# Last stage of a two-layer kernel: selection by partition quadrants in two halves, with the first half's ranks as sums of signs

## The chip, the cores and the metric

The kernel runs on one core of a Trainium2 chip. A core has a matrix engine (PE, TensorE), a vector engine (DVE, VectorE), an activation engine (ACT, ScalarE), a general engine (POOL, GpSimd) and a synchronising engine (SP, SyncE). Each works through its own list of instructions in order, and they wait for one another through semaphores. Transfers are issued from SP, ACT or POOL and carried out by shared DMA engines. The metric is the device time of one execution in microseconds (us), median of several runs; lower is better.

## The reference

Four sequences of 1024 tokens with 256 numbers each pass through two layers: windowed attention, a mixture of eight experts with two chosen per token, full attention with its own normalisation, and at last the stage that is changed here. That stage lets each of 8 experts choose 128 of the 1024 tokens of each sequence:

```python
B, N, D = x.shape
E = gate_w.shape[-1]
M = N // E
gate_logits = jnp.einsum('bnd,de->bne', x, gate_w)
competitive_gates = sinkhorn(gate_logits)
vals, idx = jax.lax.top_k(jnp.swapaxes(competitive_gates, -1, -2), M)
...
routed = x[b_idx, routed_indices]
...
outputs = jnp.einsum('ebmd,edf->ebmf', routed, experts)
outputs = outputs * jnp.transpose(gate_values, (2, 0, 1))[..., None]
vals_bmed = jnp.transpose(outputs, (1, 2, 0, 3))
routed_back = jnp.zeros_like(x).at[b_idx, routed_indices].set(vals_bmed)
```

`sinkhorn` divides the gates eight times by their sums over tokens and over experts. The input is normalised per token before the stage, and `x` is added to `routed_back` after it. Where several experts have chosen one token, the last one's row is what is kept; the kernel takes the highest expert number.

## The kernel before

The tokens are 32 tiles of 128, held in `x_t`. The last stage treats the sequences in two groups of two: group 0 is tiles 0 to 15, group 1 tiles 16 to 31. A group has 16 pairs of (sequence, expert), called columns here, and each column chooses 128 tokens.

For each group these steps follow. `gate_steps` (L1014) normalises the tiles, writes them to `xn_d` in DRAM for later gathers, turns them on PE and multiplies by the gate weights. `share_steps` (L1064) does the eight rounds of division. `choose_steps` (L1088) copies the gates to `by_tile`, turns them so that each column is one partition of `cur` (16 partitions of 1024 numbers), and then runs 16 rounds on DVE. A round has three instructions: the eight largest values (L1109, `max`), their places (L1111, `max_index`), and a copy in which they are struck out (L1115, `match_replace`). Values and places are turned back, so that slot s of a column lies on partition s (`slot_gate`, `slot_tok`, `slot_row`).

`experts_on` (L1135) gathers the rows of each column by an indirect DMA from POOL into `xg`, turns them (L1181, copied by ACT at L1185), multiplies by the expert's matrix (L1154), scales by the gate on ACT (L1164) and writes them to `y_d` from SP (L1168). To return the results, each token must know its slot. For group 0 the slots are scattered to `rank_d` in DRAM by `ranks` (L1585 and after) while attention still runs. For group 1 they are made on chip: DVE compares each place with the chosen token (L1832, `hot`), and PE multiplies this with slot numbers, `slot_col` (L1834). `back` (L1194) turns the slots into row numbers, gathers the rows of `y_d` into `yr` (L1225, POOL), adds `x` (L1231, POOL for group 0, DVE for group 1) and writes the output from SP (L1232).

Group 0's gates and selection are steps of a generator that is interleaved with the second attention: after each half of an attention step, `some` takes a step of the waiting jobs, and a selection step only if nothing else was done or at every fourth attention step. `finish` normalises the attention's results, the last tile's too (L1559 to L1564, on POOL). Group 1's gates complete only when the last attention tile is through. The last stage then runs group 1's division and selection, with group 0's experts and returns beside it, and then group 1's experts, ranks and returns.

Each engine's order is made by a scheduler from its own estimate of times, within the orders that the code demands. `paced` adds a wait on another instruction; `issue_after` asks for a place behind another one. Hardware DMAs, issued from SP and ACT alike, take turns on eight semaphores in the scheduled order, and the compiled order shows a wait for the transfer that used the same semaphore before. POOL's DMAs have eight of their own.

Of the kernel before, what the change touches and what calls it, by code (L numbers as in the profile page):

```python
# [8 lines left out]
F32 = mybir.dt.float32  # L9
# [30 lines left out]
def two_layers(  # L40
# [521 lines left out]
    with ExitStack() as lc:  # L562
# [30 lines left out]
        for k in range(2):  # L593
            t = pool.tile([P, D], F32, tag="yr0", name="sb3_k", bufs=7)
            nc.gpsimd.dma_start(out=t, in_=sb3[k].partition_broadcast(P))
            if k == 0:
                nc.gpsimd.tensor_scalar(sb3_b, t, 0.5, None, ALU.mult)
            else:
                nc.gpsimd.tensor_scalar(t, t, 0.5, None, ALU.mult)
                nc.gpsimd.tensor_tensor(sb3_b, sb3_b, t, ALU.add)  # L600
# [413 lines left out]
    def gate_steps(i0: int, i1: int, bank, lag: int):  # L1014
# [7 lines left out]
        for t in range(i0, i1):  # L1022
            xn = gpool.tile([P, D], F32, tag="xng", name="xng", bufs=4)
            nc.gpsimd.tensor_scalar(
                xn, x_t[t], mv_all[:, t, 0:1], rstd_all[:, t : t + 1], ALU.subtract, ALU.mult
            )
            nc.gpsimd.dma_start(out=xn_d[t // TB][(t % TB) * P : (t % TB + 1) * P, :], in_=xn)
            xns.append(xn)
            yield 0
# [58 lines left out]
    def choose_steps(g: int, bank, chosen, after):  # L1088

        by_tile = gpool.tile([P, TB, GE], F32, tag="by_tile", name="by_tile", bufs=1)  # L1090
        nc.vector.tensor_copy(
            by_tile.rearrange("p t (b e) -> p t b e", b=GB),
            gates[:, g * GT : (g + 1) * GT, :].rearrange("p (b t) e -> p t b e", b=GB),
        )
        yield 0
        cur = gpool.tile([GE, S], F32, tag="cur", name="cur")
        for hf in range(2):
            ps = bank()
            for t in range(TB // 2):
                nc.tensor.transpose(  # L1100
                    ps[:GE, t * P : (t + 1) * P], by_tile[:, hf * TB // 2 + t, :], ident
                )
            nc.vector.tensor_copy(cur[:, hf * 512 : (hf + 1) * 512], ps[:GE, :])
            yield 1
        top_v = gpool.tile([GE, CAP], F32, tag="top_v", name="top_v", bufs=1)
        top_i = gpool.tile([GE, CAP], U32, tag="top_i", name="top_i", bufs=1)
        for k in range(CAP // 8):
            eight = slice(8 * k, 8 * k + 8)
            nc.vector.max(out=top_v[:, eight], in_=cur)  # L1109
            yield 0  # L1110
            nc.vector.max_index(out=top_i[:, eight], in_max=top_v[:, eight], in_values=cur)  # L1111
            yield 0
            if k < CAP // 8 - 1:
                nxt = gpool.tile([GE, S], F32, tag="cur", name="cur")
                nc.vector.match_replace(  # L1115
                    out=nxt, in_to_replace=top_v[:, eight], in_values=cur, imm_value=-1.0
                )
                cur = nxt
                yield 0
        top_f = gpool.tile([GE, CAP], F32, tag="top_f", name="top_f", bufs=1)  # L1120
        nc.vector.tensor_copy(top_f, top_i)
        ps = bank()
        nc.tensor.transpose(ps[:, :GE], top_v, ident[:GE, :GE])
        nc.tensor.transpose(ps[:, GE : 2 * GE], top_f, ident[:GE, :GE])
        slot_gate = gpool.tile([P, GE], F32, tag="slot_gate", name="slot_gate", bufs=1)
        nc.vector.tensor_copy(slot_gate, ps[:, :GE])
        slot_tok = gpool.tile([P, GE], F32, tag="slot_tok", name="slot_tok", bufs=1)
        nc.vector.tensor_copy(slot_tok, ps[:, GE : 2 * GE])
        slot_row = gpool.tile([P, GE], I32, tag="slot_row", name="slot_row", bufs=1)
        nc.vector.tensor_copy(slot_row, slot_tok)  # L1130
        chosen[g] = slot_gate, slot_tok, slot_row
        after()
        yield 1

    def experts_on(g: int, pool, chosen, w_all, beside=None):  # L1135

        slot_gate, _, slot_row = chosen[g]
        rows = {}

        def gather(m: int):  # L1140
            for n in (2 * m, 2 * m + 1):
                xg = rows[n] = pool.tile([P, D], F32, tag="xg", name="xg", bufs=6)
                nc.gpsimd.indirect_dma_start(
                    out=xg[:, :],
                    out_offset=None,
                    in_=xn_d[g * GB + n // E][:, :],
                    in_offset=bass.IndirectOffsetOnAxis(ap=slot_row[:, n : n + 1], axis=0),
                )

        def product(m: int, xgT):  # L1150
# [10 lines left out]
            for h in range(2):  # L1161
# [6 lines left out]
                nc.sync.dma_start(out=y_d[g * GB + b][e * CAP : (e + 1) * CAP, :], in_=yg)  # L1168


        gather(0)
        gather(1)
        last = None
        for m in range(GE // 2 + 1):
            if m < GE // 2:
                ps = one_bank()
                for h in range(2):
                    xg = rows.pop(2 * m + h)
                    for kc in range(2):
                        c = (2 * h + kc) * P  # L1180
                        nc.tensor.transpose(  # L1181
                            ps[:, c : c + P], xg[:, kc * P : (kc + 1) * P], ident
                        )
                xgT = pool.tile([P, 4, P], F32, tag="xgT", name="xgT", bufs=3)
                nc.scalar.copy(xgT.rearrange("p k t -> p (k t)"), ps)  # L1185
                if m + 2 < GE // 2:
                    gather(m + 2)
                if beside is not None:
                    beside(m)
# [4 lines left out]
    def back(g: int, rank, order: str, queue, rows):  # L1194
# [3 lines left out]
        def t3(name):  # L1198
            return gpool.tile([P, GT, E], F32, tag=name, name=name, bufs=1)
# [3 lines left out]
        nc.vector.tensor_tensor(key, key, expert_no.to_broadcast([P, GT, E]), ALU.add)  # L1203
        best = gpool.tile([P, GT, 1], F32, tag="best", name="best", bufs=1)
        nc.vector.tensor_reduce(best[:, :, 0], key, AX.X, ALU.max)
        nc.vector.tensor_tensor(key, key, best.to_broadcast([P, GT, E]), ALU.is_equal)
        nc.vector.tensor_tensor(rank, rank, first_slot.to_broadcast([P, GT, E]), ALU.add)
        nc.vector.tensor_tensor(key, key, rank, ALU.mult)
        taken = gpool.tile([P, GT], F32, tag="taken", name="taken", bufs=1)
        nc.vector.tensor_scalar(taken, best[:, :, 0], E - 0.5, None, ALU.is_gt)  # L1210
        src_f = gpool.tile([P, GT], F32, tag="src_f", name="src_f", bufs=1)
# [6 lines left out]
        src_row = gpool.tile([P, GT], I32, tag="src_row", name="src_row", bufs=1)  # L1218
        nc.vector.tensor_copy(src_row, src_f)
        for j in range(GT):  # L1220
            b, t = divmod(j, TB)
            n = j if order == "bt" else t * GB + b
            i = g * GT + j
            yr = rows.tile([P, D], F32, tag=f"yr{g}", name="yr", bufs=8)
            nc.gpsimd.indirect_dma_start(  # L1225
                out=yr[:, :],
                out_offset=None,
                in_=y_d[g * GB + b][:, :],
                in_offset=bass.IndirectOffsetOnAxis(ap=src_row[:, n : n + 1], axis=0),
            )  # L1230
            (nc.vector if g else nc.gpsimd).tensor_tensor(yr, yr, x_t[i], ALU.add)  # L1231
            queue.dma_start(out=out_rows[i * P : (i + 1) * P, :], in_=yr)  # L1232
# [21 lines left out]
    with ExitStack() as lc:  # L1254
# [285 lines left out]
        def finish(i0: int, ys):  # L1540
# [16 lines left out]
            for j in range(n):  # L1557
                x = x_t[i0 + j]
                nc.gpsimd.tensor_scalar(  # L1559
                    ys[j], ys[j], mv[:, j, 0:1], rstd[:, j : j + 1], ALU.subtract, ALU.mult  # L1560
                )
                nc.gpsimd.tensor_tensor(ys[j], ys[j], gamma_b, ALU.mult)
                nc.gpsimd.tensor_tensor(ys[j], ys[j], beta_b, ALU.add)
                nc.gpsimd.tensor_tensor(x, x, ys[j], ALU.add)  # L1564
# [20 lines left out]
        def ranks():  # L1585

            slot_tok = chosen[0][1]
# [68 lines left out]
        def fetch(i: int, k: int, behind=None):  # L1656

            yr = pools["yr"].tile([P, D], F32, tag="yr0", name="yr0", bufs=7)
# [134 lines left out]
    with ExitStack() as lc:  # L1793
# [6 lines left out]
        nc.gpsimd.iota(place_i, pattern=[[1, S]], base=0, channel_multiplier=0)  # L1800
# [3 lines left out]
        slot_i = wpool.tile([P, GE], I32, name="slot_i")  # L1804
        nc.gpsimd.iota(slot_i, pattern=[[0, GE]], base=1, channel_multiplier=1)
        slot_col = wpool.tile([P, GE, GE], BF16, name="slot_col")
        nc.gpsimd.memset(slot_col, 0.0)
        nc.gpsimd.tensor_copy(
            slot_col.rearrange("p n m -> p (n m)")[:, :: GE + 1], slot_i
        )  # L1810
# [4 lines left out]

        run(share_steps(1, one_bank, 0))

        choose = choose_steps(1, one_bank, chosen, lambda: None)
        for _ in range(3):
            next(choose)  # L1820
        experts_on(0, pool, chosen, w_all)
        for _ in range(24):
            next(choose)
        back(0, read_ranks(), "bt", nc.sync, pool)
        run(choose)
        rank_ps = two_banks()

        def hot_rows(e: int):
            slot_tok = chosen[1][1]
            for n in (2 * e, 2 * e + 1):  # L1830
                hot = pool.tile([P, S], BF16, tag="hot", name="hot", bufs=3)
                nc.vector.tensor_scalar(hot, place, slot_tok[:, n : n + 1], None, ALU.is_equal)  # L1832
# [56 lines left out]
```

## Time and profile before

| | us |
|---|---|
| median of 3 runs | 2508.23 (2507.6 to 2517.59) |
| profiled execution, its time | 2505.83 |
| span of its trace | 2504.1 |
| last attention output copied (L1782) | 2338.14 |
| first selection round of group 1 (L1109) | 2381.85 |
| `slot_row` of group 1 (L1130) | 2441.84 |
| first gather of group 1's return (L1225) | 2477.94 |

The last five times are positions in the trace, counted from its start. The table below is the busy time of the engines in four stretches of the end, in us, with the granted clock of PE as a share of full speed.

| stretch | PE | DVE | ACT | POOL | PE clock |
|---|---|---|---|---|---|
| 2300 to 2350 | 37.82 | 7.82 | 27.79 | 27.55 | 0.80 |
| 2350 to 2400 | 27.23 | 34.60 | 10.44 | 23.97 | 0.65 |
| 2400 to 2450 | 7.40 | 46.34 | 1.89 | 29.97 | 0.59 |
| 2450 to 2505 | 23.95 | 14.94 | 11.43 | 26.39 | 0.74 |

Read it by stretch: in the third, DVE works nearly all the time and the others little; in the fourth no engine is busy for half of it. The trace names instructions by line, engine, operation and tile. "Idle before" is the time that the engine stood still ahead of an instruction, with what released it.

### The profile page before, as it was taken

To read this page: it belongs to the slowest core of one execution; us is meant where nothing else is said; L and a number is where in the kernel's file an instruction comes from. 1 tells how busy PE (TensorE), PEld (TensorE's weight loads), DVE (VectorE), ACT (ScalarE), POOL (GpSimd) and SP (SyncE) were. 2 spreads that over 40 slices of the span, in tenths; PEclk is the share of its full clock that TensorE was granted. 3 is DMA by queue.
4 is the path that set the end of the run, shared out by engine and by line. 5 is a ranking of instruction groups with operands and counts; after the bars stand their busy time and mean duration, and the time that the engine had idled before them with its cause. 6 is when DMAs were issued, how large, how long until landed. Compare 5 with 4: busy or idle time off the path is not lost.

```text
span 2504.1 us, 42234 instructions
## 1 busy us (share of the span) xinstructions
PE 2273.6 (91%) x16844; PEld 1352.2 (54%) x16844; DVE 1392.9 (56%) x2304; ACT 985.6 (39%) x1354; POOL 632.2 (25%) x728
## 2 busy tenths in 40 slices
PE   6999999799999999999888999999999999998434
PEld 3566666566557888887444444444444444443222
DVE  5455545524321222222476877777777798995393
ACT  1333333312111222222114666666666565666311
POOL 2233333510440000000333221212122211124455
PEclk8999999899999999999999999999999999999667
DMA  3000000420116666664515221313121313100144
GB/s 93 19 11 11 11 13 9 133 74 1 66 63 200 217 206 209 213 207 156 117 44 120 59 69 45 69 45 69 45 69 45 69 44 69 44 19 11 56 122 135
DMA packets 201744, 204.90 MB, mean 82 GB/s; under 512 B 90200, under 2 KB 162392, under 8 KB 201548
## 3 DMA queue, kind: packets, MB, share of 16 engines
q1 hardware_dynamic: 179148, 162.13, 22.7%
q0 software_dynamic: 11584, 29.72, 4.0%
q10 hardware_dynamic: 10816, 10.36, 1.2%
q8 instruction: 133, 2.18, 0.4%
q14 instruction: 63, 0.52, 0.1%
HBM read 140.70 MB, written 56.96 MB: 79 GB/s over the span
## 4 chain that ended last, share of the span: by engine, by line
PE 69%; DVE 16%; issue 6%; ACT 4%; POOL 3%; DMA 3%; SPq 0%; DVEq 0%; ACTq 0%; POOLq 0%
PE two L962 10%; PE two L1471 9%; PE acc L1486 8%; PE two L717 6%; DVE tops L1436 5%; PE two L329 5%; PE two L1429 4%; PE acc L989 4%; PE two L258 3%; PE two L1351 2%; PE two L321 2%; PE acc L735 2%; PE misc L735 2%; PE acc L396 2%; PE misc L440 1%
## 5 line engine op out<-in xcount | busy, mean ns | idle before, releaser
L1436 DVE TENSOR_REDUCE tops<-two 128x2 f32<-128x1024 f32 x512 | 619.5, 1217 | 103.8 <-PE two L1429 101.6
L1479 ACT ACTIVATE pT<-two 128x1024 f32<-128x1024 f32 x512 | 523.4, 1025 | 303.7 <-PE two L1471 299.2
L1486 PE MATMUL acc<-pT,v_t 128*32 128x256 f32 x4096 | 342.7, 393 | 5.8 <-ACT pT L1479 5.6
L1471 PE MATMUL two<-q_st,k_st 64*128 64x512 f32 x1024 | 259.8, 499 | 19.3 <-ACT pT L1479 11.8
L962 PE MATMUL two<-xbT,w_t 128*128 128x256 f32 (+1 forms) x1280 | 260.0, 358 | 1.3 <-ACT xbT L951 0.7
L717 PE MATMUL two<-xnT_f,w_t 128*128 128x512 f32 x512 | 234.7, 608 | 7.4 <-DVE tops L1436 5.1
L962 PEld LDWEIGHTS two<-xbT,w_t 128*128 128x128 f32 x1280 | 224.1, 192 | 32.0 <-ACT xbT L951 5.3
L1429 PE MATMUL two<-k_st,q_st 64*128 64x512 f32 x1024 | 220.3, 403 | 4.2 <-DVE glu L726 1.6
L1471 PEld LDWEIGHTS two<-q_st,k_st 64*128 64x128 f32 x1024 | 96.8, 184 | 209.8 <-issue 118.8
L1659 POOL DMA_INDIRECT yr<-ys_d,slot x64 | 62.6, 979 | 573.5 <-DMA w_raw<-in_L_attn_wk_dram 434.7
L1471 PE MATMUL two<-top_st,minus 64*128 64x512 f32 x1024 | 206.5, 396 | 0.0
L978 DVE SCALAR_TENSOR_TENSOR glu_b<-two,b_blk,act_b 128x256 f32<-128x256 f32 (+1 forms) x160 | 72.6, 453 | 235.8 <-ACT act_b L972 235.8
L972 ACT ACTIVATE act_b<-two,b_blk 128x256 f32<-128x256 f32 (+1 forms) x160 | 72.1, 451 | 312.6 <-PE two L962 161.1
L1486 PEld LDWEIGHTS acc<-pT,v_t 128*32 128x32 f32 x4096 | 86.5, 108 | 166.1 <-issue 142.8
L717 PEld LDWEIGHTS two<-xnT_f,w_t 128*128 128x128 f32 x512 | 96.7, 195 | 116.4 <-issue 104.4
L989 PE MATMUL acc<-w_t,glu_b 128*128 128x256 f32 x568 | 148.6, 390 | 8.0 <-DVE glu_b L978 3.7
L355 DVE TENSOR_REDUCE top<-two 128x4 f32<-128x768 f32 (+1 forms) x128 | 112.5, 919 | 69.0 <-PE two L329 69.0
L381 POOL TENSOR_SCALAR_AFFINE_SELECT pT<-pT 128x1024 f32<-128x1024 f32 x64 | 70.5, 1102 | 296.5 <-ACT pT L378 296.5
L725 ACT ACTIVATE act<-two,bT 128x512 f32<-128x512 f32 x64 | 44.0, 687 | 254.0 <-PE two L717 251.2
L1429 PEld LDWEIGHTS two<-k_st,q_st 64*128 64x128 f32 x1024 | 103.2, 185 | 73.5 <-ACT pT L1479 22.0
L378 ACT ACTIVATE pT<-two 128x768 f32<-128x768 f32 (+1 forms) x128 | 93.7, 783 | 119.0 <-PE two L329 118.6
L989 PEld LDWEIGHTS acc<-w_t,glu_b 128*128 128x128 f32 x568 | 102.1, 189 | 34.7 <-DVE glu_b L978 23.3
(317 smaller groups left out, 3095.0 us busy)
## 6 DMA issues: line engine op xcount, KB each, us to landing
w_t<-in_L_ffn_rw_dram SPq DMA_DIRECT2D x120, 512.0 KB
halves<-split SPq DMA_DIRECT2D x64, 256.0 KB
q_st<-halves SPq DMA_DIRECT2D x128, 128.0 KB
k_st<-halves SPq DMA_DIRECT2D x256, 64.0 KB
xb<-xs_d SPq DMA_DIRECT2D x31, 256.0 KB
ys_d<-yb ACTq DMA_DIRECT2D x31, 256.0 KB
xs_d<-zeros SPq DMA_DIRECT2D x5, 1536.0 KB
b_t<-in_L_ffn_rb_dram SPq DMA_DIRECT2D x40, 128.0 KB
```

Of the source, the lines that this page charges most:

```text
L329: mm(parts[r][:, gg, :], lhsT=left[32 * r : 32 * r + rows, g, l0 : l0 + P], rhs=right[32 * r : 32 * r + rows, g, r0 : r0 + n], start=(mask ...
L355: nc.vector.tensor_reduce(tops[i][:, 2 * ab : 2 * ab + 2, 2 * gp : 2 * gp + 2], scs[ab], AX.X, ALU.max)
L378: nc.scalar.activation(pt[:, 2 * ab : 2 * ab + 2, :, :n], scs[ab], AF.Exp)
L717: mm(ps[:, n * 512 : (n + 1) * 512], lhsT=w_t[:, kc, f * P : (f + 1) * P], rhs=xnT[:, kc, cols], start=(kc == 0), stop=(kc == 1),)
L735: mm(ps[:, jj * D : (jj + 1) * D], lhsT=glu[:, f, j * P : (j + 1) * P], rhs=w3_t[:, f, :], start=(f == 0), stop=(f == NF - 1),)
L962: mm(ps[:, m * 512 + ff * cols : m * 512 + (ff + 1) * cols], lhsT=w_t[:, kc, f * P : (f + 1) * P], rhs=xbT[:, kc, :cols], start=(kc == 0), ...
L989: mm(ps[:, a * D : (a + 1) * D], lhsT=glu[:, f, a * P : (a + 1) * P], rhs=w3_t[:, f, :], start=(f == 0), stop=(f == NF - 1),)
L1429: mm(sc[:, hh], lhsT=q_st[rows, j * P : (j + 1) * P], rhs=k_st[rows, kk * 512 : (kk + 1) * 512], start=True, stop=True,)
L1436: newest["vector"] = nc.vector.tensor_reduce(tops[:, :, j, kk], sc, AX.X, ALU.max).ins
L1471: mm(sc[:, hh * 512 : (hh + 1) * 512], lhsT=minus[rows] if top else k_st[rows, k * P : (k + 1) * P], rhs=(top_ring[p % 2] if top else q_st ...
L1479: newest["scalar"] = nc.scalar.activation(pt, sc, AF.Exp).ins
L1486: newest["tensor"] = mm(oT_ps[32 * r : 32 * r + 32, hh * D : (hh + 1) * D], lhsT=vals[n // HU][:, n % HU, k, :], rhs=pts[r // 2][:, hh * 5 ...
```

## The change

**Selection by quadrants.** The gates are turned twice side by side, so that 32 partitions hold the 16 columns doubled. A round now reads one of 16 places (four quadrants of 32 partitions, four positions in each) and `match_replace` writes the next place. The values of every round stay, so the places are found afterwards for four rounds, or two, at once: `max_index` over 128 partitions for group 0 and 64 for a half of group 1.

**Two halves for group 1.** After eight rounds the first 64 slots of each column are turned, gathered (8 gathers, each of two columns' half) and run through `half_experts`, whose products are 64 slots wide; then the same for the other 64.

**Ranks.** For the first half ACT computes the sign of (place - token + 0.5) and PE adds these with weights of half a slot number; the difference of neighbouring places, made by four products with `ident` and `minus`, is the slot number at the chosen place. The second half's ranks are made by DVE comparisons as before and added to the same sums. They are read out per sequence.

**Moved.** Results go to `y_d` from ACT instead of SP, 16 writes for group 0 and 32 of half size for group 1. Group 0's returns are issued in three lots (7, 7, 2), each behind a lot of gathers in POOL's order. All 16 gathers of group 0's experts stand ahead of the division of group 1. The last tile's normalisation steps and its `xng` go from POOL to DVE. Buffers: `xg` 16 for 6, `yr` 16 for 8 per group, `yr0` 6 for 7.

```diff
-            nc.gpsimd.tensor_scalar(
-                xn, x_t[t], mv_all[:, t, 0:1], rstd_all[:, t : t + 1], ALU.subtract, ALU.mult
-            )
+            last_xn[:] = [
+                (nc.gpsimd if lag else nc.vector)
+                .tensor_scalar(
...
-        cur = gpool.tile([GE, S], F32, tag="cur", name="cur")
+        cur = gpool.tile([P, 4, S], F32, tag="cur", name="cur", bufs=1)
...
-        for k in range(CAP // 8):
-            eight = slice(8 * k, 8 * k + 8)
-            nc.vector.max(out=top_v[:, eight], in_=cur)
-            yield 0
-            nc.vector.max_index(out=top_i[:, eight], in_max=top_v[:, eight], in_values=cur)
-            yield 0
...
+        def of_round(k: int):
+            return slice(32 * (k // 4), 32 * (k // 4) + 32), k % 4
...
+        for k in range(rounds):
+            q, a = of_round(k)
+            behind(nc.vector.max, out=top_v[q, a, :], in_=cur[q, a, :])
             yield 0
...
+            if k + 1 < rounds:
+                q1, a1 = of_round(k + 1)
+                behind(
+                    nc.vector.match_replace,
+                    out=cur[q1, a1, :], in_to_replace=top_v[q, a, :], in_values=cur[q, a, :],
+                    imm_value=-1.0,
+                )
                 yield 0
...
+            if (k + 1) % (rounds // parts):
+                continue
+            part = (k + 1) * parts // rounds - 1
+            rows = slice(part * P // parts, (part + 1) * P // parts)
+            for a in range(4):
+                behind(
+                    nc.vector.max_index,
+                    out=top_i[rows, a, :], in_max=top_v[rows, a, :], in_values=cur[rows, a, :],
+                )
+                yield 0
+            behind(nc.vector.tensor_copy, top_f[rows], top_i[rows])
...
+                        with ExitStack() as order:
+                            if part:
+                                order.enter_context(tc.issue_after(newest["ranks"]))
+                            mm(
+                                ps[row : row + 32, k0 * n : (k0 + 1) * n],
+                                lhsT=top[q].rearrange("p a i -> p (a i)"),
+                                rhs=ident[q, 32 * j + h : 32 * j + GE : parts],
...
-                nc.sync.dma_start(out=y_d[g * GB + b][e * CAP : (e + 1) * CAP, :], in_=yg)
...
+                nc.scalar.dma_start(out=y_d[g * GB + b][e * CAP : (e + 1) * CAP, :], in_=yg)
...
+    def half_experts(g: int, part: int, m: int, xgs, pool, w_all):
...
+        for c in range(2):
+            for kc in range(2):
+                for h in range(2):
+                    half = slice(64 * h, 64 * h + 64)
+                    mm(
+                        ps[half, c * D : (c + 1) * D],
+                        lhsT=xgT[:, 2 * c + kc, half],
+                        rhs=w_all[:, (2 * (m + c) + h) % E, kc, :],
...
+            for h in range(2):
+                row = ((2 * (m + c) + h) % E) * CAP + 64 * part
+                nc.scalar.dma_start(
+                    out=y_d[g * GB + b][row : row + 64, :], in_=yg[64 * h : 64 * h + 64, :]
+                )
...
+        xgs0 = take_rows(chosen[0, 0], columns, pool)
         run(share_steps(1, one_bank, 0))
...
+        choose = choose_steps(1, one_bank, chosen, lambda: ready.append(0), 2)
+        for _ in range(4):
             next(choose)
...
+            if part:
+                nc.vector.tensor_scalar(hot, place, tok, None, ALU.is_equal)
+            else:
+                nc.scalar.activation(hot, place, AF.Sign, bias=half_less[:, m : m + 1])
...
+        some_back(7)
+        while not ready:
+            next(choose)
...
+        xgs = take_rows(chosen[1, 0], columns, pool)
+        for m in range(0, E, 2):
+            half_experts(1, 0, m, xgs[m : m + 2], pool, w_all)
+            for c in range(2):
+                ranks_of(0, m + c)
+            next(choose)
+        for b in range(GB):
+            nc.scalar.copy(sums_to[32 * b : 32 * b + E, 1:], rank_ps[32 * b : 32 * b + E, :])
...
+        some_back(7)
         run(choose)
...
+        xgs = take_rows(chosen[1, 1], columns, pool)
+        some_back(2)
...
+            for m in range(b * E // 2, (b + 1) * E // 2, 2):
+                for c in range(2):
+                    ranks_of(1, m + c)
+                half_experts(1, 1, m, xgs[m : m + 2], pool, w_all)
...
+        with tc.issue_after(newest["numbers"]):
+            for b in range(GB):
+                for t in range(TB):
+                    back(GB + b, t, src_rows[b], t, nc.vector, nc.sync, pool)
```

In the order that the scheduler makes of it, POOL has the seven first returns of group 0, then the 8 gathers of the first half, then seven returns, the 8 gathers of the second half, two returns, and the 16 returns of group 1. PE has the products that turn the second half's values and places behind the last rank product of the first half.

## Prediction

> **What bounds the kernel now.** I read the whole page first (PE is busy for 91% of the span, but the last slices show a single engine each), then the chain of waits in the last 265 us, then the engines' timelines there. The chain:
>
> ```profile
> 2381.14 0.69 DVE cur L1103
> 2381.85 1.23 DVE top_v L1109
> 2383.10 1.27 DVE top_i L1111 x2
> 2384.38 1.21 DVE cur L1115
> 2385.61 1.23 DVE top_v L1109
> ...
> 2442.17 0.76 DVE hot L1832
> ...
> 2459.23 0.96 PE two L1834 x4
> ...
> 2477.94 0.94 POOL yr L1225
> ...
> 2497.00 3.69 DMA yr<-y_d,src_row
> ```
>
> Columns are start, length, piece. From 2381.85 to 2442.0 (60.2 us) only DVE's rounds count, 3.76 us each: values, places, strike-out, about 1.25 us apiece. From there to 2477.94 (35.9) come 16 gathers, experts and ranks at 3.3 us per pair of columns. The returns end it: 16 gathers, 1.25 us apart, and 6.2 for the last to land and leave (26.2 together). What is won must come from the first two stretches.
>
> **Attention, group 0's selection.** Its 16 + 16 + 15 = 47 instructions become 16 + 15 + 4 = 35. The compiled order keeps the same slots for the first 35 and drops the last twelve. DVE is 90% busy there, but only pieces on the chain pay:
>
> ```profile
> 2243.08 1.12 DVE top_v L1109
> 2244.20 2.25 DVE tops L1436 x2
> 2246.45 0.11 DVE rec L1507
> 2246.57 1.20 DVE top_i L1111
> ```
>
> Of the twelve, three lie on it (with 2253.95): 3.5 us. The rank scatters (L1597) then come earlier; two of them, 1.06 and 1.08 us, lie on POOL's chain at 2291.87 and 2298.08. I take 1.5 of about 2.6 with their gaps. Sum **-5** (bounds -1 and -9; the small reordering where attention begins is within that).
>
> **The last tile.** On POOL its four steps and `xng` took 1.23 + 0.74 + 0.72 + 0.73 and 1.24. On DVE the rows for these shapes are 0.45 and 0.42, but the second step still waits for gates at 2350.75. That leaves -1.4, and a second copy of `by_tile` gives back 0.2. POOL's new preparation and its 16 gathers fit beside the 21 us of division. If they did not, group 0's experts would start late, beside DVE's rounds, at no loss. Group 1's first round starts at 2381.85 - 1.2 = 2380.65.
>
> **Selection alone.** First half: 8 x 2.52 + 4 x 1.25 + 0.25 = 25.5, to 2406.1. The turn on PE takes 0.65, and two instructions of the sort (2.5) stand before `slot_row`: 2408.9. Second half: 15 x 1.25 + 0.8 of small copies + 5.25 brings DVE to 2431.1, and `slot_row` could be ready at 2432.3, ten us before today. Searching 64 partitions instead of 16 costs nothing if columns set the price: L1436 takes 1.22 us for 128 x 1024, L1109 1.21 for 16 x 1024. No row shows a strike-out that writes another quadrant; 0 is taken, +0.2 each would be +6.
>
> **POOL's queue.** Seven returns with adds took 13.7 us from 2397.12 in before's timeline. Now: 7 returns from 2396.4 to 2410.0; 8 gathers to 2420.0; 7 returns to 2433.7. So POOL alone would delay the second half's gathers by only 1 us.
>
> **ACT's queue is the added wait.** The writes to `y_d` now stand among ACT's Signs and copies, and each waits for the transfer that last used its semaphore. By the compiled order these are shared with SP's output writes: the fourth write of the first half's first pair waits for the first output of the second lot of seven, later ones for its third to seventh. POOL starts that lot only at 2420.0. The nearest row is SP's queue of today:
>
> ```profile
> 2399.62 0.84 ACT L1164 ACTIVATE yg<-two,slot_gate 128x256 f32<-128x256 f32 x2 [0.85 <-ACT xgT L1185]
> ...
> 2406.16 0.87 SPq L1168 DMA_DIRECT2D y_d<-yg  x2
> ```
>
> The results were ready at 2400.5 and left at 2406.16, behind output writes; only SP stood. The Trainium skill ("DMA: Bandwidth & Descriptors", Anatomy of one DMA) says that a semaphore wait is taken by the issuing sequencer before dispatch. By this rule ACT stands, and with it the Signs behind; the row shows such a wait only on SP, where nothing was behind. Issue costs 0.37 (rows: 0.350 for SP's 128-row writes, 0.417 for ACT's larger L1003).
>
> By the rule: three Signs (1.03, as L1479) end at 2412.2, the first pair is scaled at 2418, and the fourth write stands until 2420.0 + 6.25 + 0.74 + 2.5 for landing = 2429.5. Behind it: nine writes 3.3, three Signs 3.1, two pairs of scalings 1.7, a copy 0.6, and about 1.4 of waiting for PE: 2439.6. Then a copy 0.6, two Signs 2.1 and the last rank products 1.0: **2443.3**. PE's order puts the second half's turn behind those products, so `slot_row` comes at 2443.3 + 1.2 = 2444.5, not 2432.3: **+2.5** against today's 2442.0, before the gain in attention. Without the wait the last product would be at 2433.2.
>
> **Second half to the returns.** Gathers from 2444.8 to 2454.8; two returns of group 0 to 2460.1; their outputs land at 2462.5, and the last two writes of sequence 2 wait for them, land at 2465.5. First return gather 2465.8: 21.3 us behind `slot_row` instead of 35.9, **-14.6**. Sequence 3 (writes 2472.2, row numbers 2472.7) is ready before POOL needs it at 2475.8. Returns and end: 26.2 as today.
>
> **The 64-wide products.** A call has 16 PE records:
>
> ```profile
> 2120.24 1.97 PE L1391 MATMUL misc<-wv_t,xnT_a 128*64 128x128 f32 x32
> 2122.13 0.50 PE L1471 MATMUL two<-q_st,k_st 64*128 64x512 f32 x2
> ```
>
> That is 0.053 us per 128-row record, so 0.107 at 256 rows, 1.7 us a call; L1154's pitch of 0.216 would give 3.5. "TensorEngine Tiling (Array Packing)" (Tiling Modes, Key Properties) speaks against it: changing the mode drains PE. In the row the next shape starts before the modelled end of the last. By the row 0, by the rule one record's 0.27 for each of 16 changes, 4.3 in all, half of it on the path. I take the row: gathers at 2.5 us per pair cover 1.7 + 0.6 + 1.0.
>
> **Sum.** 2504.1 + 2.5 - 14.6 = 2492.0; -5: a span of 2487.0. With the 1.7 outside the span: **2489**, against the profiled 2505.83 (the median shown is 2508.23, 0.1% above it). About 0.5%, some 12.5 us, is what can be told from no change here.
>
> **Rivals.** (A) The forecast, 0.50.
>
> (B) The semaphore waits do not bite, because the writes land earlier or the lots fall otherwise: last rank product 2433.2, POOL ready, span 2478.7 - 5, time **2475**. For it: SP's writes land in 2.4 us at best. Against: the second lot lies behind 8 gathers. 0.18.
>
> (C) Products of 64 columns run one after another with a drain (3.8 a call) and ACT's issue costs 0.5: PE and ACT set the second half, returns from 2472.7 and 2483.8, span 2500.0 - 5, time **2497**. For it: L1154's pitch and a clock of 0.59 to 0.74. Against: L1391. 0.20.
>
> (D) Slower: ACT becomes the bound by its writes. 32 of them stand in series with scalings. At 1.48 us each (SP's longest row, below) the writes of sequence 3 land at 2499.4, the returns wait, span 2516.0 - 5, time **2513**; it is slower than before from 1.25 us a write, and by over 0.5% from 1.7 (2519).
>
> ```profile
> L1168 SPq DMA_DIRECT2D y_d<-yg x32: 319/350/1478, 2386.3 to 2474.8; - x32
> L1003 ACTq DMA_DIRECT2D ys_d<-yb x40: 352/417/427, 783.9 to 1186.1; - x40
> ```
>
> (min/median/max in ns.) Against: ACT's own row never exceeds 0.43. 0.12.
>
> **Numbers.** Range 2474 to 2506: B and C whole, the bounds of attention, a strike-out at +0.2; D is left out. Faster takes most of A, all of B and some of C: 0.64. Same: the rest of A and most of C, half of D: 0.27. Slower: the upper part of D and what I do not see: 0.09.
>
> **What would show it.** In the new trace: 31 instructions 1.25 us apart without `max_index` between; ACT idle for about 11 us behind its fourth half-size write, released by an output DMA; the second half's turn released by a rank product and not by DVE; first return gather 21 us behind the second `slot_row`; calls of 1.7 us on PE. Attention should end about 5 us earlier. I am wrong if ACT does not stand there (B), if PE's products set the pace (C), or if a write on ACT costs over 1.2 us (D).

## The result: 0.4% slower, and the profile after

The changed kernel took 2521.95 us (median of 20 runs, 2510.13 to 2535.43); the kernel before took 2509.39 on the same chip (20 runs). The ratio is 1.0045, with a 95% interval from 1.0028 to 1.0062. The forecast was 2489, in a range from 2474 to 2506. Run once more beside other kernels (e6 below), the ratio was 1.0040 (1.0021 to 1.0059), so the loss of some 10 us is clear of the noise, though small.

The profiled execution of the changed kernel took 2526.09 us, its span is 2524.0. I cut both traces at two marks that both have: the first and the last of the 32 copies to `oT` in the attention stage (L1782 before, L1865 after).

| | before | after | after, again (e6) |
|---|---|---|---|
| start to first `oT` copy | 1367.4 | 1380.2 | 1371.4 |
| attention: first to last `oT` copy | 970.8 | 980.1 | 979.9 |
| last stage: last `oT` copy to the end | 166.0 | 163.7 | 163.6 |

The first row holds almost no changed code, and over all the profiles below it lies anywhere between 1354.9 and 1380.2: it is noise of single executions (e1 to e3, which leave that code alone, have 1362 to 1364 there). The other two rows repeat within 0.2 us in these two traces; attention does not always (986.0 in e3, with the same order of instructions; see there). So in these traces **attention is 9 us longer and the last stage only 2 us shorter**; the forecast had -5 and -12. The two add up to 7 us, the low end of what the times over all runs say (7 to 16).

The last stage first. These are lines of the chain of waits of the changed kernel (start, length, piece; the sort of group 1 begins at 2403.67):

```profile
2403.67 1.23 DVE top_v L1132
2404.92 1.29 DVE cur L1132 x2
...
2452.10 0.33 SPq L1313
...
2452.84 2.19 DMA out_dram<-yr
2455.11 0.48 ACTq L1270
...
2472.55 7.04 PE two L1973 x8
2479.59 1.80 PE two L1949 x4
...
2497.53 0.33 POOL yr L1306
```

The rounds of the sort are shorter, as meant (2.57 us each, with no index search between). But the chain doesn't stay on VectorE: it goes through an output write of SP, a `y_d` write of ACT, and eight products on TensorE (L1973, the difference of the sums) before the returns begin. ACT's own timeline shows the first of these (start, length, engine, line; in brackets the idle time of the engine before, its DMA issues counted as idle, and what ended it):

```profile
2444.45 8.00 ACTq L1270 DMA_DIRECT2D y_d<-yg  x4
2452.50 1.15 ACT L1946 ACTIVATE hot<-place,half_less 128x1024 bf16<-128x1024 f32 x1 [7.71 <-DMA out_dram<-yr]
```

Four writes take 8.0 us, because one of them waits for an output of the second lot of returns to land. At the median of 0.61 us for the issue of such a write (last section), some 2.4 of the 8.0 are issue and 5.6 the wait. ACT computes nothing for 7.71 us ahead of the Sign behind it, and the rank products and the second half's turn stand behind the Sign. The forecast had this wait in it. What it hadn't is in the attention stage.

There, let a *pair* be the time from one `oT` copy to the next. Most of the 31 pairs agree to 0.3 us. These don't, besides 7, 11 and 15:

| pair | before | after | e4: group 0 chosen whole | e9: attention of before |
|---|---|---|---|---|
| 1 + 2 | 56.4 | 58.7 | 58.7 | 56.4 |
| 23 | 41.9 | 44.0 | 43.5 | 41.9 |
| 24 + 25 + 26 | 89.7 | 93.8 | 89.7 | 89.7 |
| 27 + 28 | 61.7 | 59.8 | 62.9 | 61.7 |
| 29 + 30 + 31 | 94.1 | 94.2 | 94.0 | 94.0 |

(Pairs 7, 11, 15 and 23 jump by some 1.5 us between executions of the same code, so one such jump proves nothing. The jumps go with the granted clock: pair 7 took 38.97 us at a clock of 1.00 before and 40.57 at 0.96 after, pair 11 took 40.44 at 0.96 before and 39.04 at 1.00 after. Pair 23 had 1.00 before and 0.96 after; e4, with 0.96 there too, took 43.5 without any quadrants, so most of pair 23's +2.1 is clock.) In pairs 22 to 28 VectorE does group 0's selection beside the attention's row maxima. Pairs 24 to 26, before and after, in one line each (start:end length, busy time and number of instructions of each engine, granted clock of PE, DMA):

```profile
core 0: us, PE busy (x) PEld busy (x) DVE busy (x) ACT busy (x) POOL busy (x), PEclk, DMA share, GB/s
2092.65:2182.33 89.68, 83.70 (x772) 39.16 (x770) 83.68 (x113) 57.60 (x65) 23.19 (x28) 1.00 0.18 47
2112.49:2206.31 93.82, 84.24 (x772) 39.17 (x770) 86.88 (x111) 57.63 (x65) 23.19 (x28) 1.00 0.17 45
```

The clock is full in both. VectorE is busy 3.2 us longer with *fewer* instructions, TensorE hardly longer, and TensorE's weight loads wait for VectorE's maxima for 14.4 us instead of 9.6. VectorE's timeline of the changed kernel, early and late in this selection, shows why:

```profile
2066.23 1.23 DVE L1517 TENSOR_REDUCE tops<-two 128x2 f32<-128x1024 f32 x1 [0.25 <-PE two L1510]
2067.37 1.20 DVE L1132 MAX8 top_v<-cur 32x8 f32<-32x1024 f32 x1
2068.51 1.20 DVE L1517 TENSOR_REDUCE tops<-two 128x2 f32<-128x1024 f32 x1
...
2116.93 2.35 DVE L1517 TENSOR_REDUCE tops<-two 128x2 f32<-128x1024 f32 x2
2119.30 1.22 DVE L1132 MAX8 top_v<-cur 32x8 f32<-32x1024 f32 x1
2120.55 1.23 DVE L1517 TENSOR_REDUCE tops<-two 128x2 f32<-128x1024 f32 x1
```

Add start and length. The reduction at 2066.23 ends at 2067.46, and the max began at 2067.37: they overlap by 0.09 us, and so do the next two (0.06). Fifty us later, with the same shapes, the reduction ends at 2119.28 and the max starts at 2119.30; the max ends at 2120.52 and the next starts at 2120.55. The overlap has turned into a gap, on both sides. Over all 35 selection instructions it is sharp: the first seven, on partitions 0 to 31, have -0.07 before and behind; from the eighth (the first strike-out that writes partitions 32 to 63) to the 31st nearly every one has +0.03 on both sides; the four index searches at the end, which start on partition 0 again, have -0.08 behind them. The Trainium skill ("VectorE: DVE Perf Modes", Two Vector instructions with no wait between them) has the rule: an instruction whose input or output starts in another quadrant of 32 partitions than the last one that used that memory is held until all earlier ones have finished. The gaps agree. The neighbours here start at partition 0, so each selection instruction in quadrants 1 to 3 is held, and so is what follows. As an estimate from the gaps, 24 instructions x 2 x 0.105 = 5 us of VectorE. Pairs 24 to 26 have 16 of the 24, 3.4 us; VectorE was busy 3.2 us longer there, and the pairs grew by 4.1.

### The profile page after: what moved, and what is told of

It is laid out like the page before. It is cut to its first block, busy times and chain, and to the rows that moved or that the text cites. A ratio compares the mean times of both kernels' runs of the same rounds, so it can differ in the third digit from the quotient of the medians.

```text
span 2524.0 us, 42458 instructions
## 1 busy us (share of the span) xinstructions
PE 2306.4 (91%) x16968; PEld 1362.4 (54%) x16968; DVE 1377.0 (55%) x2276; ACT 997.9 (40%) x1369; POOL 629.3 (25%) x730
## 5 line engine op out<-in xcount | busy, mean ns | idle before, releaser
L1510 PEld LDWEIGHTS two<-k_st,q_st 64*128 64x128 f32 x1024 | 103.6, 186 | 80.1 <-ACT pT L1560 21.3
```

What stands on the lines that cost most here:

```text
L1510: mm(sc[:, hh], lhsT=q_st[rows, j * P : (j + 1) * P], rhs=k_st[rows, kk * 512 : (kk + 1) * 512], start=True, stop=True,)
```

## The experiments

Theory H: the loss is made of these holds in attention and of losses in the last stage (ACT's wait, and the eight products). Rival C: it is the granted clock, or something that no edit of these parts moves. Each ratio is against the kernel before on the same chip, with its 95% interval.

| | attention | last stage | ratio |
|---|---|---|---|
| e1 writes on SP | 981.3 | 160.2 | 1.0049 (1.0030 to 1.0067) |
| e2 difference on VectorE | 981.4 | 160.8 | 1.0027 (1.0013 to 1.0042) |
| e3 both | 986.0 | 154.6 | 1.0022 (1.0004 to 1.0039) |
| e4 group 0 whole | 976.6 | 164.3 | 1.0030 (1.0016 to 1.0043) |
| e5 e3 with attention of before | 970.9 | 159.8 | 0.9963 (0.9943 to 0.9983) |
| e7 e4 on partitions 32 to 47 | 989.5 | 167.1 | 1.0061 (1.0039 to 1.0083) |
| e8 before, six `yr0` | 974.4 | 166.6 | 1.0011 (0.9987 to 1.0035) |
| e9 after, attention of before | 970.8 | 164.2 | 1.0003 (0.9988 to 1.0018) |
| e10 e9, writes on SP, turn first | 970.8 | 152.7 | 0.9944 (0.9925 to 0.9964) |
| e11 e5, subtraction later | 970.9 | 149.1 | 0.9931 (0.9904 to 0.9958) |
| e12 e11, eight `yg` | 973.6 | 149.7 | 0.9949 (0.9928 to 0.9970) |
| e13 before, 16 KB `cur` | 973.4 | 166.2 | 1.0028 (1.0004 to 1.0052) |

### e1: `y_d` writes back on SP

```diff
-                nc.scalar.dma_start(out=y_d[...
+                nc.sync.dma_start(out=y_d[...
```

> The changed kernel, with every y_d write (16 whole ones of group 0, 32 half ones of group 1) issued by SP again instead of ACT. Theory L (last stage: the forecast gain is given back there, most of it by ACT): the 8.0 us that ACT stands at a y_d write and the 0.6 us of each issue go, so the last rank product of the first half ends some 10 us sooner, slot_row of the second half follows the selection's own end (about 53 us after the first Max instead of 65.3), and the time falls by 8 to 12 us against the changed kernel, to about the time before. Rival C (the loss is granted clock or sits in the attention stage, and the last stage has other cover): less than 3 us. Rival S (SP's queue now stands at output writes, and the y_d writes behind them come late): no gain or a loss, with y_d writes landing later than now.

The last stage lost 3.5 us, not 8 to 12, and the time didn't move. ACT did stop standing at output writes, and the sums were ready for L1973 at 101.7 us after the last `oT` copy instead of 112.2. But the planner had now put the eight products *ahead* of the second half's turn on TensorE, so `slot_row` came at 109.4 us after the last copy, as before the edit (108.8). The test was spoilt by an order that the edit moved; e10 holds that order fixed.

### e2: the difference taken on VectorE

```diff
-        for hf in range(2):
-            for k, one in enumerate((ident, minus)):
-                mm(rank_ps[:RB, ...], lhsT=one[:RB, :RB], rhs=sums_to[...], ...)
+                if m == 0:
+                    step = pool.tile([RB, S], F32, tag="step", name="step", bufs=1)
+                    nc.vector.tensor_tensor(step, sums_to[:, 1:], sums_to[:, :S], ALU.subtract)
...
-            nc.scalar.copy(rankT[mine], rank_ps[mine, :])
+            nc.vector.tensor_tensor(rankT[mine], rank_ps[mine, :], step[mine], ALU.add)
```

> The changed kernel, with the 8 true-fp32 products by ident and minus (7.04 us on TensorE in the trace) replaced by one subtraction on VectorE of the sums at two neighbouring columns, added to the second half's counts at the read-out (by VectorE instead of ScalarE's copy). Same result. Theory L: TensorE is free 7 us sooner for the second half's experts; of that 3 to 6 us reach the end, as the gathers of the second half (10.0 us) and ScalarE's 16 half writes then bound it. Rival C: under 2 us.

2.9 us of last stage, at the edge of what was expected. ACT stood 7.33 us as in the changed kernel, and `slot_row` stayed at 108.7.

### e3: both

> Both edits together: y_d writes on SP, and the subtraction on VectorE instead of 8 products. Theory L: the two losses follow one another on one chain (ACT, then TensorE), so they add: 12 to 17 us under the changed kernel, which is 2 to 6 us under the kernel before. Rival C: within 3 us of the changed kernel.

The last stage lost 9.1 us, more than e1 and e2 together, though less than the 12 to 17 expected; the time stayed above the kernel before, since attention still carried its loss. Its 986.0 is 5.9 us more than in the changed kernel, with the same order of instructions on TensorE, VectorE, ACT and POOL: in pairs 23 to 28 VectorE was busy 174.74 us against 174.20, but the granted clock was 0.94 against 0.99 and TensorE was busy 192.23 against 183.62. So one trace's attention can differ by 6 us by the clock alone. One more wait showed on VectorE:

```profile
2441.28 1.24 DVE L1132 FIND_INDEX8 top_i<-top_v,cur 64x8 uint32<-64x1024 f32 x1
2450.14 1.22 DVE L1980 TENSOR_TENSOR step<-sums_to 40x1024 f32<-40x1024 f32 x1 [7.62 <-ACT sums_to L1967]
2451.39 0.18 DVE L1132 CAST top_f<-top_i 64x32 f32<-64x32 uint32 x1
```

My subtraction was planned ahead of the cast that ends the sort, and VectorE stood 7.62 us for sums that the sort has no need of. e11 mends that.

### e4: group 0 chosen whole again

```diff
-                    choose_steps(0, misc_bank, chosen, chose)
+                    choose_whole(0, misc_bank, chosen, chose)
```

(`choose_whole` is the `choose_steps` of before, in the space of the new `cur`.)

> The changed kernel, with group 0's selection (the one inside the attention stage) done as before: 16 rounds of max, place and strike-out on 16 partitions, 47 VectorE instructions instead of 35; group 1 and all else as in the changed kernel. My forecast's step (12 fewer instructions give 5 us): 5 us slower than the changed kernel. Theory A (the quadrant form costs the attention stage about 9 us, as the intervals between pairs in the two profiles seem to say): 7 to 10 us faster. Theory N (VectorE's selection has cover in the attention stage, and the difference of the profiles is clock): within 2 us.

Attention fell from 980 to 976.6, and the ratio from 1.0040 to 1.0045 down to 1.0030: between Theory N and Theory A, and against the forecast's step. Pairs 24 to 26 went back to 89.7 us, the value of before; pairs 27 and 28 gave 3.1 back, as the twelve more instructions run there (1.9 by the kernel before, 61.7; the rest is clock: 0.97 there in e4, 1.00 in the other two). Pairs 1 and 2 kept their 58.7.

### e7: the same on other partitions

```diff
-        cur = both[:GE, 0, :]
+        cur = both[32 : 32 + GE, 0, :]
```

(and `top_v`, `top_i`, `top_f` likewise)

> e4 (group 0 chosen whole, 47 instructions) with nothing changed but the partitions: the 16 rows and their tops stand on partitions 32 to 47 instead of 0 to 15. Theory H (an instruction that starts in another quadrant than its neighbours starts only when they have ended, and so does the one behind it): the gap in front of and behind nearly all 47 turns from -0.07 us to +0.03, 47 x 2 x 0.10 = 9 us of VectorE, and pairs 23 to 28, where VectorE is busy over 90%, get some 5 to 9 us longer than in e4. Rival (the quadrant form loses by its semaphores, its strike-out in place or its 32 rows): gaps and pairs as in e4.

This is the decisive pair. The two kernels have the same instructions in the same stage, and differ by 32 partitions. VectorE's timeline in e4:

```profile
2102.36 0.40 DVE L1676 BATCH_NORM_STATS2 st<-y 128x6 f32<-128x256 f32 x1
2102.69 1.20 DVE L1206 MAX8 cur<-cur 16x8 f32<-16x1024 f32 x1
2103.82 0.15 DVE L1677 BATCH_NORM_AGGREGATE mv<-st 128x2 f32<-128x6 f32 x1
```

and the same three in e7:

```profile
2122.33 0.40 DVE L1676 BATCH_NORM_STATS2 st<-y 128x6 f32<-128x256 f32 x1
2122.77 1.22 DVE L1206 MAX8 cur<-cur 16x8 f32<-16x1024 f32 x1
2124.02 0.18 DVE L1677 BATCH_NORM_AGGREGATE mv<-st 128x2 f32<-128x6 f32 x1
```

From first to third start it is 1.46 us in e4 and 1.69 in e7. Attention grew by 12.9 us, more than the 5 to 9 expected. Pairs 23 to 28 show why, e4 first and e7 below:

```profile
2044.40:2240.48 196.08, 185.41 (x1548) 86.87 (x1548) 176.31 (x234) 118.64 (x134) 30.06 (x36) 0.98 0.17 44
2062.57:2272.57 210.00, 191.89 (x1548) 89.36 (x1548) 184.92 (x234) 118.62 (x134) 30.16 (x36) 0.95 0.16 41
```

VectorE is busy 8.6 us longer, close to the 9 us of holds. TensorE is busy 6.5 us longer for the same products, and the clock fell from 0.98 to 0.95: as an estimate, 0.05 x 210 less 0.02 x 196 is 6.6 us of clock lost, which leaves some 7 of the 13.9 us by which these pairs grew. The times over all runs say the same: the two ratios differ by 0.0031, some 8 us, though their intervals leave 1 to 14. The gaps go with the quadrant and not with the semaphores, the strike-out or the number of rows, which e4 and e7 share.

The clock in pairs 23 to 28 is 0.94 to 0.99 in the six traces with holds there (after, e1 to e3, e6, e7) and 0.98 to 1.00 in the others. Whether the holds bring it down or chance does, no run tried.

### e8 and e13: pairs 1 and 2

```diff
-            yr = pools["yr"].tile([P, D], F32, tag="yr0", name="yr0", bufs=7)
+            yr = pools["yr"].tile([P, D], F32, tag="yr0", name="yr0", bufs=6)
```

> The kernel before with one edit: six yr0 buffers instead of seven (the change gave one up for the larger cur). Theory Y (the second pair of the attention stage, 28.1 us before and 32.0 us in every kernel with six, waits for a yr0 buffer): pairs 1 and 2 together 58.8 us instead of 56.4, time up by 2 to 3 us. Rival: pairs 1 and 2 as before, the cause is another.

Pairs 1 and 2 stayed at 28.3 and 28.1: the buffer isn't the cause. e13 is e8 with `bufs=4` on `cur` as well (16 KB instead of 8):

> The kernel before with four cur buffers (16 KB, as the quadrant form takes) and six yr0 buffers (e8 had these six alone, and pairs 1 and 2 of the attention stage stayed at 56.4 us). Theory M (the 2.4 us more in pairs 1 and 2, which e1 to e4, e6 and e7 show and e5, e8 to e12 don't, come from the larger cur: the attention stage's tiles lie elsewhere, and the planner puts TensorE's products there in another order): pairs 1 and 2 take 58.8 us; the selection's own pairs 23 to 28 stay within 2 us of before; time up by 2 to 3 us. Rival: pairs 1 and 2 at 56.4 us, and the cause is in another part of the change.

Pairs 1 and 2 took 26.8 and 32.0 us, exactly as in the changed kernel, and pairs 23 to 28 stayed at before's values (193.0 against 193.3). So these 2.4 us go with the *size* of `cur` alone. TensorE's products come in another order in the stage's first pairs; that its other tiles lie elsewhere is my reading, and why that order is worse wasn't tried.

### e5 and e9: attention as before, last stage as in e3 or as changed

```diff
-    def choose_steps(g: int, bank, chosen, after, parts: int = 1):
+    def choose_steps(g: int, bank, chosen, after, gpool, parts: int = 1):
...
-        choose = choose_steps(1, one_bank, chosen, lambda: ready.append(0), 2)
+        choose = choose_steps(1, one_bank, chosen, lambda: ready.append(0), wpool, 2)
```

(with `choose_whole` for group 0 in 8 KB, and seven `yr0`)

> The last stage of e3 (y_d writes on SP, the subtraction on VectorE instead of 8 products) behind the attention stage of the kernel before: group 0 chosen whole on 16 partitions, seven yr0 buffers; group 1's quadrants get their space in the last stage's own pool. Theory H (the quadrant form holds VectorE in the attention stage, the last stage gains once ACT and TensorE are freed): attention 971 us from the first oT copy to the last as before (981 to 986 in e1 to e3), last stage about 155 us (166 before), so 9 to 12 us under the kernel before, ratio about 0.9955. Rival C (clock decides, edits don't): within 0.1% of e3, ratio 1.002.

> The changed kernel with the attention stage of the kernel before (group 0 chosen whole in an 8 KB cur, seven yr0 buffers; group 1's quadrants take their space in the last stage's pool), the last stage untouched: y_d writes on ACT, 8 difference products on TensorE. Theory H: attention 971 us instead of 980, last stage 163.6 as in the changed kernel, so 9 us under it and within 3 us of the kernel before (ratio 0.999 to 1.001). Rival (the attention edit only moves the loss into the last stage): attention 971, last stage over 168, time as the changed kernel.

e9 came as Theory H had it. It has the changed last stage whole, and its attention is 970.8: ratio 1.0003. So the **whole measured loss of the change goes with its edits of attention**, and its last stage is worth about nothing (164.2 against 166.0). e5 beats the kernel before, and its attention came as expected, but its last stage took 159.8 us and not 155. The order on TensorE, ACT and POOL in that stage is that of e3 (154.6). In e5 ACT stood once for 6.99 us, released by nothing that the trace names, and VectorE's subtraction then 12.07 (7.62 in e3):

```profile
2432.19 0.84 ACT L1312 ACTIVATE yg<-two,slot_gate 128x256 f32<-128x256 f32 x2 [6.99 <-remote]
```

No other trace has this stop; its cause is open. e6 is the changed kernel again on e5's chip:

> The changed kernel itself once more, on the same chip as the other three of this group. Theory H: the first 1360 us, where its code is that of before, take what they take before (the 11 us more of its first profile were that one execution's clock); ACT stands some 8 us at a y_d write in the last stage again; attention again 980 us or more. Rival C: the first 1360 us are again 10 us longer.

Its first stretch was 4 us longer than in the trace of before, and not 13, while attention and ACT's wait (7.78 us) came again to 0.2 us. With e9 this leaves Rival C no room as the whole cause: the loss goes when the edits go. It does have a share: the changed kernel's trace has the jump of the clock in pairs 7, 15 and 23, the trace of before in pair 11 alone, so some 3 us of attention's +9.3 are clock.

### e10: writes on SP, the turn ahead of the products

e9, with e1's edit, and the eight products held behind the turn:

```diff
+        with tc.issue_after(newest["turn"]):
+            for hf in range(2):
+                for k, one in enumerate((ident, minus)):
...
```

> e9 with y_d writes on SP, and the 8 difference products placed behind the second half's turn on TensorE (in e1 they came ahead of it, which hid what ACT's wait cost). Theory H: with ACT not standing, the first half's rank products end near 101 us after the last oT copy instead of 108, so slot_row of the second half at about 102.5 us (108.9 in the changed kernel); the products' 7 us then stand partly beside the gathers; last stage 156 to 159 us (163.6), ratio about 0.997. Rival: slot_row stays at 108 to 109 us, so it wasn't ACT that held the turn.

Better than expected: `slot_row` at 96.5 us (110.0 in e9), last stage 152.7 (164.2). Taking the writes out of ACT's queue gives 11.5 us, wait and issue together; the planner also moved some Signs on ACT and rank products on TensorE. The forecast had reckoned 10.1 us for the wait (2443.3 against 2433.2). The wait is now on SP, where the first half-size writes stand behind five outputs and nothing else does:

```profile
2401.25 21.95 SPq L1360 DMA_DIRECT2D out_dram<-yr  x5
2423.29 2.45 SPq L1317 DMA_DIRECT2D y_d<-yg  x4
```

TensorE's timeline (matmuls alone) shows where the products went:

```profile
2425.58 0.22 PE L1167 MATMUL misc<-ident,top_f 32*32 32x8 f32 x8
2432.81 1.93 PE L2023 MATMUL two<-sums_to,ident 40*40 40x512 f32 x2 [7.00 <-ACT sums_to L2016]
```

The turn leaves first; the products stand beside the gathers of the second half.

### e11 and e12: a version that beats both

```diff
+                    with tc.issue_after(newest["slots"]):
+                        nc.vector.tensor_tensor(step, sums_to[:, 1:], sums_to[:, :S], ALU.subtract)
```

(`newest["slots"]` is the last copy to `slot_row`; e12 has `bufs=8` on `yg` besides.)

> e5 with one order more: the subtraction on VectorE comes behind slot_row of the second half. In e3 and e5 it stood ahead of the cast to top_f and VectorE stood 7.6 us there, waiting for ScalarE's copy of the sums. Theory H: slot_row of the second half at about 95 to 101 us after the last oT copy (107.6 in e5), last stage 150 to 155 us (159.8), ratio 0.992 to 0.995. Rival: the rank products (TensorE's order puts the turn behind them) hold slot_row at 105 us or later, gain under 2 us.

> e11 with eight yg buffers instead of four. In e3 ScalarE stood 3.2 us and three times 0.8 us at yg, waiting for a y_d write to end, in each half, with the copies behind it. Theory H: those waits go, slot_row some 3 to 5 us sooner and the last rank copy 3 us sooner, last stage 146 to 150 us, ratio about 0.990. Rival: y_d writes and POOL's 16 return gathers bound the end, gain under 2 us against e11.

e11: `slot_row` at 95.5 us, last stage 149.1, median 2490.43 us against 2506.74: 0.7% faster than before. Of the 10.7 us under e5, about half is what e5 lost against e3; against e3 the last stage is 5.5 us shorter and `slot_row` 7.4 us earlier. Its trace's last stage is 3.6 us shorter than e10's, and the medians of the two are 0.6 us apart, so with the turn ahead of them the eight products cost little. e12 is a miss: ACT no longer waits for a `yg`, but SP now issues 15 half-size writes in a row in 9.6 us, and the last of them lands no sooner. The rival had it.

## Why the prediction was wrong, step by step

- **What bounds the kernel**: right. The sort, the chain from `slot_row` to the first return, and the returns made up the last stage after the change too.
- **Attention, -5: the step that failed.** It became +9.3. The forecast let the twelve dropped instructions pay 3.5 us on VectorE's chain and 1.5 on POOL's. Measured: pairs 27 and 28 lost 1.9 us, pairs 29 to 31 nothing. Against that stand pairs 24 to 26 with +4.1 at full clock (the holds), pairs 1 and 2 with +2.3 (`cur`'s size), pair 23 with +2.1 and the rest with +2.6; of these last 4.7, some 3 are two more dips of the clock. The forecast weighed writing another quadrant only for the strike-out, in the last stage, and took 0 "for it", with no term for the instructions around it in attention. For the last stage the 0 was nearly right (rounds of 2.57 us against 2.52), for in a sort that runs alone the instructions have a gap already: before, the first max ends at 2381.85 + 1.23 = 2383.08 and the search starts at 2383.10. Beside other work the price falls on both neighbours. (Its "+0.2 each would be +6" counts all 31 instructions; the 15 strike-outs alone would be 3.) The reordering at the start of attention was put "within" the bounds of this step; it alone was half as large as the gain claimed.
- **The last tile, -1.2**: measured -0.4 (43.7 to 43.3 us from the last `oT` copy to the first round). Too small to matter.
- **Selection alone**: right to a us. First `slot_row` 28.9 us after the first round (28.25 forecast), VectorE's end at 50.9 (50.45).
- **ACT's queue**: right in mechanism, and in the sum partly by luck. The fourth write stood, released by an output of the second lot, at about 2452, which is 48.3 us after the first round against 48.85 forecast. But ACT had the first pair scaled 3.8 us later than forecast (41.1 against 37.35), so it stood some 5.6 us and not 11, and its writes took 0.61 us to issue where 0.37 was reckoned. The two errors nearly cancel: second `slot_row` 65.3 us after the first round against 63.85. e9 to e10 shows that the writes on ACT are a cause and not a bystander. It agrees with what the forecast took from the Trainium skill ("DMA: Bandwidth & Descriptors", Anatomy of one DMA): a wait is taken by the engine that issues. The section treats POOL's path; here it held on ACT's, and what was behind stood too.
- **Second half to the returns, 21.3 us**: the second failing step, by size. It measured 28.6. The sum had no term for the eight difference products, 7.04 us between the second half's turn and its rank products; e2, without them, has 24.8, so they cost some 4 of the 7.3 us missing, and the gathers hide the rest of them. The other 3 us are not isolated: the issue of ACT's writes at 0.61 us instead of 0.37 is one candidate, but e3, without the products and with the writes on SP, is no shorter than e2 (25.2).
- **Products of 64 columns, 1.7 us a call**: the row was the right choice. Six of the eight calls took 1.90 to 1.95 us at a granted clock of 1.00, the other two 3.10 at 0.61 and 3.68 at 0.50. So the price of 3.8 in Rival C was nearly met once, by the clock and not by a drain. Nor did the rule that the forecast took from the Trainium skill ("TensorEngine Tiling (Array Packing)", Tiling Modes, Key Properties) apply: it speaks of a change of mode and excepts a change of tile, and the products of a call all have 64 columns and only change their place.
- **Returns, 26.2**: 26.5.

So of a forecast of -17 us, 14 were lost in attention and 10 in the last stage. Rival B (no wait) had 140.6 us for the last stage (2478.7 less 2338.1); e10, where ACT doesn't wait, has 152.7. Rival C had 161.9, the nearest to 163.7, but for another reason, products with a drain. Rival D's price of a write wasn't reached (0.87 at most). The slower side was thought of as a mishap in ACT's queue, and came through VectorE in a stage that was taken as a small gain.

## What to carry to other kernels

Before work is spread over partition quadrants, look at what runs between its instructions: beside neighbours that start on partition 0, each one in another quadrant cost two lost overlaps here, some 0.2 us together, and where the others wait for that engine most of it reached the time. Spread a chain that runs alone, and keep one that is threaded through other work in the quadrant of that work. A DMA write belongs on a queue behind which nothing urgent stands, and a helper that needs a late input must be ordered behind what doesn't; in this kernel these two were worth 11.5 us (e9 to e10) and some 5 (e3 to e11) of the last stage, as much as the whole idea.

## What the runs showed of the hardware that I hadn't expected

- Two independent VectorE instructions overlap by 0.06 to 0.09 us when all start in one quadrant, and have a gap of 0.02 to 0.04 us when one doesn't. 47 instructions moved by one quadrant made VectorE busy for 8.6 us longer (e4 to e7).
- A write of half the size takes *longer* to issue in this kernel. ACT's rows for DMAs in the changed kernel (min/median/max ns; L1270 writes 64 rows, L1232 writes 128):

```profile
L1270 ACTq DMA_DIRECT2D y_d<-yg x32: 452/607/874, 2444.5 to 2502.9; - x32
L1232 ACTq DMA_DIRECT2D y_d<-yg x16: 326/364/445, 2407.6 to 2426.3; - x16
```

  On SP the half-size ones take 573 ns at the median (e11), so it isn't ACT's doing; why it is so wasn't tried. Cutting 16 writes into 32 more than trebles the issue time, from 16 x 0.36 to 32 x 0.61 us.
